# Layer 1's edges by pairs of groups, with PSUM banks given by hand and the last groups in conditional blocks

## The chip, the core and the metric

The program runs on one core of a Trainium2 chip. The core has a matmul engine (TensorE; PE in the profile, its weight loads PEld), a vector engine (VectorE, DVE), an activation engine (ScalarE, ACT), a general engine that also gathers (GpSimd, POOL), and a sync engine that issues transfers (SyncE, SP). They run side by side, each through its own instructions in order, and meet at semaphores. Matmul results land in PSUM, eight banks of 512 f32 columns on 128 partitions; everything else lives in SBUF.

The metric is the device time of one execution in microseconds. Three timed runs of the kernel before took 2873.72, 2878.11 and 2884.48 us; the median is 2878.11.

## The reference

Four layers, each a graph layer and a feed-forward layer, on 1250 nodes of 512 features, 20000 edges, f32. Only two parts bear on the change. Layer 0's graph layer is a convolution that here goes through the matrix of edge counts between nodes. Layer 1's is an attention over edges with four heads:

```python
h = (x @ W).reshape(n, H, C)
a_src = (h * att_src[None]).sum(-1)
a_dst = (h * att_dst[None]).sum(-1)
alpha = a_src[src] + a_dst[dst] + a_edge
alpha = jax.nn.leaky_relu(alpha, NEG_SLOPE)
amax = jax.lax.stop_gradient(jax.ops.segment_max(alpha, dst, num_segments=n))
ex = jnp.exp(alpha - amax[dst])
denom = jax.ops.segment_sum(ex, dst, num_segments=n)
att = ex / (denom[dst] + 1e-16)
msg = h[src] * att[:, :, None]
out = jax.ops.segment_sum(msg, dst, num_segments=n).reshape(n, H * C) + bias
```

The sources are drawn evenly. The destinations are drawn as `1250 * uniform ** 2` and sorted, so low-numbered nodes get most of the edges.

## The kernel before, in words

**Groups.** `grouped` sorts the edges into groups of `GS` = 512, none of which crosses the border between two blocks of `P` = 125 destination nodes. There are ten blocks (`NT`); the number of groups of each depends on the data, so the program has room for `NG` = 49 groups, and a block's last group is filled up with records that match no node. Groups past the last real one are all filler; they run like the others. For each group `bgrp` holds the number of its block, which engines read into a register. `ES` holds the records (source, destination, edge features), four to a partition and group; SyncE loads them group by group, with 49 transfers of 16 KB, and only then the big part of X.

`grouped` has a conditional block already (L1933 and L1934: a value is loaded into a register of GpSimd, VectorE and TensorE, and the block is skipped if it is zero). It is skipped when the destinations come sorted, as they do.

**Counts, in `l0_gnn`.** For each group VectorE compares destination and source with a row of node numbers (`onehots`, L202 and L205), and TensorE multiplies the two (`counted`, L211) into three PSUM banks that run on over all groups; ScalarE copies the running state (L216). Between the groups stand the statistics of the node features (`stats`, L219 and L220, VectorE, one of ten blocks at groups 8 to 17), `scales` at group 18, and the projection of a block (`projected`, L231 to L240) at every third group from 21 on. The order of this stage is not given by hand: a planner in the framework orders each engine's instructions by the program's order and by when it expects their inputs.

**Edges, in `l1_edges`.** For each group:

- `gathers` (L389 by a helper): GpSimd gathers 512 rows of the table `t1` (four times 128 rows) into `G`, one of six buffers.
- `onehot` (L1614), `pieces` (L1622 to L1628): VectorE makes the one-hots of the destinations and splits the source part of the score into three bf16 pieces, in `CD` beside the bits of the destination.
- `turned`: TensorE turns `CD` (L1635) and the one-hots (L1638); ScalarE copies both out (L1640, L1642).
- `spread` (L1650), `maxima` (L1657 to L1669): TensorE spreads the scores of a head over nodes and edges, VectorE takes the maximum over a group's edges per node and head, updates the running maximum `AM`, and makes `co`, the factor by which older sums shrink.
- `fetched` (L1677), `weights_of` (L1684 to L1688): TensorE brings the maximum back to the edges, VectorE and ScalarE form `ex`.
- `scaled` (L1694, L1697): a quarter of `G` is multiplied by `ex` on VectorE, three quarters on ScalarE.
- `summed` (L1704), `added` (L1713): TensorE sums per node into two banks, VectorE shrinks and adds into `ACC`.

The loop at the end of the function writes out the order in which VectorE, ScalarE and TensorE take these steps for groups at different stages (`manual_schedule`). Each step takes its PSUM banks from a rotation of eight, nine banks a group.

**Around it.** `wst`, a pool of four 8 KB buffers a partition, streams weights for all layers and stands open over the whole program. `l1_start` prepares the edges while layer 0's feed-forward part runs; `l1_gnn` runs the edges, then divides, normalises and routes on.

Of the kernel before, what the change touches and what calls it, by code (L numbers as in the profile page):

```python
# [27 lines left out]
NG = 49  # L28
# [7 lines left out]
class Net:  # L36
# [5 lines left out]
    def __init__(self, ctx, tc, a):  # L42
# [3 lines left out]
        self.wst = ctx.enter_context(tc.tile_pool(name="wst", bufs=4))  # L46
        c = self.consts = ctx.enter_context(tc.tile_pool(name="consts", bufs=1))
        self.flip = 0
# [20 lines left out]
    def pool(self, ctx, name, bufs=1, side=None):  # L69
        return ctx.enter_context(self.tc.tile_pool(name=name, bufs=bufs, side=side, reuse_waits="tile"))  # L70

# [81 lines left out]
    def l0_gnn(self, done):  # L153
# [6 lines left out]
        with ExitStack() as ctx:  # L160
# [6 lines left out]
            with ExitStack() as c2:  # L167
# [76 lines left out]
                for g in range(NG):  # L244
                    if g % 8 == 1:
                        local(g + 1, min(g + 9, NG))
                    if g + 1 < NG:
                        onehots(g + 1)
                    counted(g)
                    if g == 0:  # L250
                        arrived()
                    if 8 <= g < 8 + NT:
                        stats(g - 8)
                    if g == 8 + NT:
                        scales()
                    if g > 18 and g % 3 == 0 and g // 3 - 7 < NT:
                        projected(g // 3 - 7)
# [344 lines left out]
    def l1_start(self, ctx):  # L602
# [11 lines left out]
        f.norm = Norm(self, ctx, "g1n", side="right", bufs=2)  # L614
# [4 lines left out]
        nc.gpsimd.dma_start(wet, a["L1_gnn_W_edge"])  # L619
        wa = p.tile([128, 4, 2 * nh], F32, name="g1wa")  # L620
# [66 lines left out]
    def l1_gnn(self, nxt):  # L687
# [3 lines left out]
        ACC = self.g1.ACC  # L691
        with ExitStack() as c2:
            self.l1_edges(c2)
        done = self.l1_route(nxt)
# [845 lines left out]
    def edge_bits(self):  # L1540
# [9 lines left out]
        with ExitStack() as c3:  # L1550
# [15 lines left out]
            bt = r.tile([128, nb], F32, name="g1bt")  # L1566
            for b in range(nb):
                y = r.tile([128, ST], I32, name=f"g1y{b}")
# [17 lines left out]
    def l1_edges(self, ctx):  # L1586
# [8 lines left out]
        gq = self.pool(ctx, "g1g", bufs=6)  # L1595
        q4 = self.pool(ctx, "g1h", bufs=4)
        q = self.pool(ctx, "g1s", bufs=3)

        st = {}

        def gathers(g):
            G = gq.tile([128, 4, tw], F32, name="G")
            ix, o = SI, 4 * g
            if g in (2, 3):

                ix, o = q.tile([128, 4], I32, name="ix"), 0
# [5 lines left out]
        def onehot(g):  # L1612
            oh = q4.tile([128, 4, P], F32, name="oh")
            nc.vector.tensor_tensor(oh, self.iota[:, None, :P].to_broadcast([128, 4, P]),  # L1614
                                    ES[:, 4 * g:4 * g + 4, 1:2].to_broadcast([128, 4, P]), OP.is_equal)
            st[g]["oh"] = oh

        def pieces(g):

            t0, v = 4 * g, st[g]  # L1620
            s = q4.tile([128, 4, nh], F32, name="s")
            nc.vector.tensor_tensor(s, v["G"][:, :, nh * (ch + 1):], AE[:, t0:t0 + 4, :], OP.add)  # L1622
            c = [CD[:, t0:t0 + 4, nr + j * nh:nr + (j + 1) * nh] for j in range(3)]
            nc.vector.tensor_copy(c[0], s)
            rest = q.tile([128, 4, nh], F32, name="rest")
            nc.vector.tensor_tensor(rest, s, c[0], OP.subtract)
            nc.vector.tensor_copy(c[1], rest)
            nc.vector.tensor_tensor(c[2], rest, c[1], OP.subtract)  # L1628
            v["s"] = s

        def turned(g):
            t0, v = 4 * g, st[g]
            pc = self.psum.tile([128, 1024], BF16, name="cd_ps", tag="b")
            for k in range(4):
                nc.tensor.transpose(pc[:nr + 3 * nh, k * 128:(k + 1) * 128], CD[:, t0 + k, :], identb)  # L1635
            ps = self.bank("oht_ps")
            for k in range(4):
                nc.tensor.transpose(ps[:P, k * 128:(k + 1) * 128], v["oh"][:, k, :], self.ident)  # L1638
            R = q.tile([nr + 3 * nh, GS], BF16, name="R")
            nc.scalar.copy(R, pc[:nr + 3 * nh, :GS])  # L1640
            ohT = q.tile([P, GS], F32, name="ohT")
# [552 lines left out]
```

## Time and profile before

| | |
|---|---|
| median of three runs | 2878.11 us |
| lowest, highest | 2873.72, 2884.48 us |
| profiled execution, its own time | 2880.85 us |
| its span, first to last instruction | 2879.0 us |
| PE busy | 2526.9 us (88%) |
| DVE busy | 1501.2 us (52%) |
| ACT busy | 834.5 us (29%) |
| POOL busy | 495.3 us (17%) |
| mean granted clock of PE | 0.91 |
| ES loads, first to last issue | 20.65 to 75.4 us |
| counts, first to last matmul | 25.0 to 192.8 us |
| edges, first gather to the first instruction behind the loop | 850.4 to 1312.5 us |

Busy times are of the whole span and say little of a stage; the shares of a stage are read from the view of busy time by stretches, and the order of events in a round from the timeline. In the timeline a square bracket says how long the engine stood idle before the instruction, and what released it. The granted clock is the share of full speed at which the throttle lets TensorE run; a matmul at half clock takes about twice as long.

### The profile page before, as it was taken

What the parts mean: (1) busy time and instruction counts of PE and PEld (TensorE: products, weight loads), DVE (VectorE), ACT (ScalarE), POOL (GpSimd) and SP (SyncE); (2) the same over time, 40 slices, a digit from 0 to 9 for tenths busy, and PEclk for the clock granted to TensorE, in tenths of its full rate; (3) what the DMA queues carried; (4) which work ended last, traced back from release to release, by engine and by line L of the source; (5) the groups of instructions that cost most, each with busy time, mean ns of one, the idle gap of its engine ahead of it and who ended that gap; (6) DMA issues with size and microseconds to landing.
All of it is one profiled execution on the core that took longest, in us unless ns stands there. A gap on an engine that the chain in (4) does not pass through costs nothing. (4 is left out here: it accounts for less than half of the span.)

```text
span 2879.0 us, 30656 instructions
## 1 busy us (share of the span) xinstructions
PE 2526.9 (88%) x10610; PEld 1598.9 (56%) x10610; DVE 1501.2 (52%) x3571; ACT 834.5 (29%) x1855; POOL 495.3 (17%) x550
## 2 busy tenths in 40 slices
PE   6799879999787888887769899999999799859896
PEld 3455679999645666665544455445544334445442
DVE  8676632000146888886234998547963554631000
ACT  4451011121124555554122244013421221211110
POOL 0012111120014444430220000100000111122211
PEclk9999679999886888887789899999999899979998
DMA  1212336666424444440773210401122202259997
GB/s 35 92 36 77 88 125 200 207 211 200 115 67 130 119 119 120 119 90 26 259 253 122 71 36 24 141 32 37 64 65 88 81 0 64 83 196 357 361 372 250
DMA packets 109897, 369.50 MB, mean 128 GB/s; under 512 B 35040, under 2 KB 39925, under 8 KB 87467
## 3 DMA queue, kind: packets, MB, share of 16 engines
q1 hardware_dynamic: 60875, 257.91, 25.5%
q0 software_dynamic: 44848, 101.55, 13.8%
q10 hardware_dynamic: 4015, 8.06, 0.9%
q8 instruction: 84, 1.38, 0.2%
q14 instruction: 75, 0.61, 0.1%
HBM read 337.83 MB, written 29.53 MB: 128 GB/s over the span
## 5 line engine op out<-in xcount | busy, mean ns | idle before, releaser
L1076 PE MATMUL g_acc<-g_e,g2hh 125*128 125x417 f32 (+1 forms) x960 | 345.3, 520 | 7.5 <-DVE g_e L1066 7.5
L1076 PEld LDWEIGHTS g_acc<-g_e,g2hh 125*128 125x128 f32 x960 | 183.1, 192 | 167.3 <-issue 157.7
L389 POOL DMA_INDIRECT G<-t,SI x188 | 186.1, 990 | 345.0 <-issue 284.9
L1704 PE MATMUL ac_ps<-G,oh 128*125 128x258 f32 x784 | 230.2, 457 | 0.0
L1704 PEld LDWEIGHTS ac_ps<-G,oh 128*125 128x125 f32 x784 | 175.7, 230 | 58.7 <-PE mx_ps L1650 20.1
L1518 PE MATMUL f_ps<-f3wd,f3ht 128*39 128x512 f32 (+1 forms) x704 | 177.0, 619 | 26.2 <-DMA f3wd<-in_L_ffn_W_down_dram 26.0
L536 PE MATMUL f_acc<-f0ht,f0w 128*128 128x187 f32 x1024 | 169.1, 328 | 13.5 <-ACT f0ht L528 13.5
L1697 ACT ACTIVATE G<-G,ex 128x129 f32<-128x129 f32 x588 | 177.7, 389 | 1.7 <-ACT ex L1688 0.2
L536 PEld LDWEIGHTS f_acc<-f0ht,f0w 128*128 128x128 f32 x1024 | 167.0, 194 | 14.1 <-ACT f0ht L528 13.8
L525 PE MATMUL f_ps<-f0xgt,f0w 128*128 128x187 f32 x1024 | 168.6, 324 | 0.1
L525 PEld LDWEIGHTS f_ps<-f0xgt,f0w 128*128 128x128 f32 x1024 | 165.3, 191 | 0.4 <-DVE f0xgt L95 0.3
L1060 DVE SCALAR_TENSOR_TENSOR g_e<-g_qb,g_a 125x1250 f32<-125x1250 f32 x80 | 120.4, 1515 | 68.4 <-DMA g_qb<-g_qd 60.8
L1524 DVE TENSOR_SCALAR f3y<-f_ps,f3k_wsel 39x512 f32<-39x512 f32 x32 | 24.0, 749 | 247.1 <-PE f_ps L1518 246.6
L1061 ACT ACTIVATE g_e<-g_e,g_a 125x1250 f32<-125x1250 f32 x80 | 106.2, 1335 | 137.9 <-DVE g_e L1060 137.7
L211 PE MATMUL c_ps<-ohs,ohd 128*125 128x512 f16 (+1 forms) x588 | 115.4, 348 | 28.3 <-DVE ohs L205 14.1
L1032 PE MATMUL g_ps<-g22w,g2ht 128*125 128x512 f32 x320 | 137.8, 592 | 0.0
L1003 DVE CUSTOM_DVE_ANT_0 g_junk<-g_mb,g_asb 125x1250 f32<-125x1250 bf16 x80 | 116.6, 1457 | 20.1 <-DMA g_asb<-g_as 16.6
L1518 PEld LDWEIGHTS f_ps<-f3wd,f3ht 128*39 128x39 f32 (+1 forms) x704 | 44.7, 120 | 141.7 <-issue 97.7
L1657 DVE TENSOR_REDUCE gm<-mx_ps 125x1 f32<-125x512 f32 x196 | 121.3, 680 | 2.4 <-PE oht_ps L1638 2.4
L1066 DVE SCALAR_TENSOR_TENSOR g_e<-g_e,CT 125x1250 f32<-125x1250 f32 x80 | 115.8, 1450 | 7.3 <-ACT g_e L1061 7.1
L549 DVE TENSOR_SCALAR f0y<-f_ps,f0xg,f0r 128x512 f32<-128x512 f32 (+1 forms) x16 | 12.2, 802 | 203.6 <-PE f_ps L547 203.6
L211 PEld LDWEIGHTS <-ohd 128*125 128x125 f16 x588 | 74.8, 139 | 69.5 <-issue 29.1
(655 smaller groups left out, 4029.4 us busy)
## 6 DMA issues: line engine op xcount, KB each, us to landing
f3wd<-in_L_ffn_W_down_dram SPq DMA_DIRECT2D x64, 1280.0 KB
f0w<-in_L_ffn_w_dram SPq DMA_DIRECT2D x64, 1024.0 KB
f1w<-in_L_ffn_w_dram SPq DMA_DIRECT2D x17, 1024.0 KB
f3wu<-in_L_ffn_W_up_dram SPq DMA_DIRECT2D x16, 1024.0 KB
g_mb<-mbd POOLq DMA_DIRECT2D x40, 305.2 KB
g_qb<-g_qd SPq DMA_DIRECT2D x16, 625.0 KB
f2tv<-in_L_ffn_tv_W_dram SPq DMA_DIRECT2D x16, 512.0 KB
wa_w<-in_L_gnn_WT_dram SPq DMA_DIRECT2D x6, 1024.0 KB
```

Source lines behind the costliest of these rows:

```text
L211: nc.tensor.matmul(pss[i][:P, :cn], lhsT=ohd[g % 2][:, k, :], rhs=ohs[(4 * g + k) % R][:, c0:c0 + cn], start=g == 0 and k == 0, stop=k == ...
L389: self.nc.gpsimd.indirect_dma_start(out=out, out_offset=None, in_=table, in_offset=bass.IndirectOffsetOnAxis(ap=idx, axis=0))
L525: nc.tensor.matmul(ps[:, :cap], lhsT=w[:, k, f * 128:(f + 1) * 128], rhs=xgt[e][:, k, :], start=k == 0, stop=k == 3)
L536: nc.tensor.matmul(acc[e][d][:, :cap], lhsT=w[:, f, d * 128:(d + 1) * 128], rhs=ht[e][:, 4 * c + f, :], start=c == 0 and f == 0, stop=c == ...
L1003: nc.vector.tensor_tensor_reduce(junk, mb, asb[h], 1.0, -3e38, OP.add, OP.max, accum_out=mx[:, i, h:h + 1])
L1032: nc.tensor.matmul(ps[:P, :], lhsT=HT[:, k, i * P:(i + 1) * P], rhs=ws[hf][k // 4][:, k % 4, :], start=k == 0, stop=k == kt - 1)
L1060: nc.vector.scalar_tensor_tensor(e, qb[h][0], A8[:, s, h:h + 1], qb[h][1], OP.add, OP.max)
L1076: nc.tensor.matmul(accs[h][f][c][:, :cn], lhsT=H[:, s, h * 256 + f * 128:h * 256 + (f + 1) * 128], rhs=e[:, c0:c0 + cn], start=s == 0, sto ...
L1518: nc.tensor.matmul(ps[64 * h:64 * h + k, :], lhsT=ht[g][:n, f, j * k:(j + 1) * k], rhs=ws[h][:n, f - f0, :], start=f == 0, stop=f == nf - 1)
L1657: nc.vector.tensor_reduce(gm[:, h:h + 1], v["mx"][h][:P, :], AX.X, OP.max)
L1697: nc.scalar.activation(gv[:, k, h], gv[:, k, h], AF.Copy, scale=v["ex"][:, k, h:h + 1])
L1704: nc.tensor.matmul(v["ac"][j][:P, 0:2 * (ch + 1)], lhsT=v["oh"][:, k, :], rhs=v["G"][:, k, j * 2 * (ch + 1):(j + 1) * 2 * (ch + 1)], start ...
```

## The change

1. `NG` becomes 50 and a new `NM` is 46. The loop of the counts runs over 46 groups; groups 46 to 49 stand behind it in a conditional block (`rest`), which is entered only if there are more than 46 groups (`more`, two new VectorE instructions in `grouped`). The same for the edges.
2. In the counts the statistics stand at groups 14 to 23, `scales` at 24, the projections at every second group from 26 on.
3. In the edges the loop runs over 23 pairs of groups. Banks are given once: four for the maxima, two for the sums (`ac`), one for the codes of both groups (`pc`), one for the turned one-hots (`tr`); what `fetched` brings back (`mg`) lies in columns 320 to 383 of the first `ac` bank. `pieces`, `coded`, `lowered` and `weights_of` work on a pair at once; `maxima` has two VectorE instructions fewer, and `co` is made by Relu and Exp on ScalarE. Of a pair's eight quarters VectorE scales one and ScalarE seven. `G` has nine buffers.
4. `wst` closes before the edges and opens again behind them (`wst2`), and the norm of `l1_start` closes as well; `edge_bits` takes two buffers in turn.

```diff
-NG = 49
+NG = 50
+NM = 46
...
+    def stream(self, name):
+        self.wctx = ExitStack()
+        self.wst = self.pool(self.wctx, name, bufs=4)
...
-                for g in range(NG):
+                for g in range(NM):
...
-                    if g + 1 < NG:
+                    if g + 1 < NM:
                         onehots(g + 1)
                     counted(g)
                     if g == 0:
                         arrived()
-                    if 8 <= g < 8 + NT:
-                        stats(g - 8)
-                    if g == 8 + NT:
+                    if 14 <= g < 14 + NT:
+                        stats(g - 14)
+                    if g == 14 + NT:
                         scales()
-                    if g > 18 and g % 3 == 0 and g // 3 - 7 < NT:
-                        projected(g // 3 - 7)
+                    if g > 25 and g % 2 == 0 and g // 2 - 13 < NT:
+                        projected(g // 2 - 13)
+                ET = mybir.EngineType
+                with self.rest([ET.PE, ET.DVE, ET.Activation]):
+                    for g in range(NM, NG):
+                        onehots(g)
+                        counted(g)
...
+        self.g1.ctx.close()
+        self.wctx.close()
         with ExitStack() as c2:
             self.l1_edges(c2)
+        self.stream("wst2")
...
+        gq = self.pool(ctx, "g1g", bufs=9)
+        q8 = self.pool(ctx, "g1h", bufs=8)
+        q4 = self.pool(ctx, "g1p", bufs=4)
+        q = self.pool(ctx, "g1s", bufs=2)
+        mx = [self.bank(f"mx_ps{h}") for h in range(nh)]
+        ac = [self.bank(f"ac_ps{j}") for j in range(2)]
+        pc = self.psum.tile([128, 1024], BF16, name="cd_ps", tag="b")
+        tr = self.bank("oht_ps")
+        mg = ac[0][:, 320:320 + 16 * nh].rearrange("p (k h) -> p k h", k=8)
...
+        def maxima(g):
+            v, w = st[g], pr[g // 2]
+            if "co" not in w:
+                w["co"] = q4.tile([P, 2, nh], F32, name="co")
+            gm = q.tile([P, 1, nh], F32, name="gm")
+            for h in range(nh):
+                nc.vector.tensor_reduce(gm[:, 0, h:h + 1], mx[h][:P, :], AX.X, OP.max)
+            b = v["b"] = nc.vector.value_load(self.bgrp[0:1, g:g + 1], min_val=0, max_val=NT - 1)
+            M = AM[:, ds(b, 1), nh:]
+            nc.vector.tensor_tensor(gm, gm, AM[:, ds(b, 1), 0:nh], OP.add)
+            nc.vector.scalar_tensor_tensor(gm, gm, 0.2, gm, OP.mult, OP.max)
+            nc.vector.tensor_tensor(w["co"][:, g % 2:g % 2 + 1, :], gm, M, OP.subtract)
+            nc.vector.tensor_tensor(M, M, gm, OP.max)
+            mn = v["mn"] = q4.tile([P, 1, 2 * nh], F32, name="mn")
+            nc.vector.tensor_copy(mn, AM[:, ds(b, 1), :])
...
+            for i in range(-2, NP + 1):
+                if i >= 0:
+                    for j in range(2):
+                        one(gathers, i + 3, j)
+                one(spread, i + 1, 0)
+                at(weights_of, i)
+                one(scaled, i, 0, range(1, 4))
+                one(maxima, i + 1, 0)
+                one(scaled_v, i, 0, 0)
+                one(summed, i - 1, 0)
+                one(spread, i + 1, 1)
+                one(added, i - 1, 0)
+                one(scaled, i, 1, range(0, 2))
+                one(turned, i + 1, 0)
+                one(scaled, i, 1, range(2, 4))
+                one(summed, i - 1, 1)
+                one(maxima, i + 1, 1)
+                if i < 0:
+                    ...
+                else:
+                    at(pieces, i + 2, 0, 2)
+                    for j in range(2):
+                        one(onehot, i + 2, j)
+                one(turned, i + 1, 1)
+                at(coded, i + 2)
+                for j in range(2):
+                    one(fetched, i + 1, j)
+                at(lowered, i + 1)
+                one(added, i - 1, 1)
+        with self.rest([E.PE, E.DVE, E.Activation, E.Pool]):
+            for i in range(NP, NG // 2):
+                ...
+    def rest(self, engines):
+        E = mybir.EngineType
+        flag = self.nc.values_load(self.more[0:1, 0:1], engines=engines, min_val=0, max_val=NG - NM)
+        return self.tc.If(flag != 0)
...
+        nc.vector.tensor_tensor(self.more, start[0:1, NT - 1:], ng[0:1, NT - 1:], OP.add)
+        nc.vector.tensor_scalar(self.more, self.more, NM, -NM, OP.max, OP.add)
```

## The prediction

> **What bounds the kernel now.** Three stages of one core are touched: the counts of layer 0 (25 to 194 us of the span), layer 1's edges (850.4, the first gather, to 1312.5, the first instruction behind the loop: 462.1 us), and what little lies between them. I read the 40 slices first (edges at DVE 8 or 9 tenths, PE 8 or 9, clock 8 or 9), then the busy time by stretches. The columns are stretch, length, then busy us of PE, PEld, DVE, ACT, POOL with their counts, granted clock, DMA share, GB/s.
>
> ```profile
> 950.00:1000.00 50.00, 43.77 (x200) 32.48 (x200) 42.09 (x147) 30.08 (x94) 21.07 (x23) 0.86 0.45 120
> 1000.00:1050.00 50.00, 43.52 (x201) 32.57 (x202) 40.57 (x144) 27.35 (x83) 21.58 (x22) 0.83 0.42 112
> 1050.00:1100.00 50.00, 42.70 (x196) 32.26 (x196) 42.76 (x148) 29.95 (x94) 22.19 (x23) 0.86 0.46 127
> ```
>
> No engine is full; PE runs at a mean 0.86 of its clock. 890 to 1300 us hold 46 groups: 410/46 = 8.91 us a group. The chain of waits in those 410 us says who hands over to whom (total, times, longest):
>
> ```profile
> PEld L1635 <- DVE g1cd L1628: 73.4, 40, 4.0
> PE cd_ps L1635 <- DVE g1cd L1628: 57.4, 34, 3.6
> DVE ex L1684 <- PE mg_ps L1677: 23.7, 40, 1.6
> DVE g1acc L1713 <- PE ac_ps L1704: 5.1, 6, 1.2
> ```
>
> DVE makes a group's pieces, PE waits for them, turns them, fetches the maxima, DVE waits for those. A group's pieces in the timeline (start, length, engine, line, operation), one group at half clock and the next at full:
>
> ```profile
> 1005.86 5.28 PE L1704 MATMUL ac_ps<-G,oh 128*125 128x258 f32 x16
> ...
> 1010.74 1.57 DVE L1713 SCALAR_TENSOR_TENSOR g1acc<-g1acc,co,ac_ps 125x129 f32 x4
> 1011.06 0.40 PE L1635 MATMUL cd_ps<-g1id,g1cd 128*27 128x128 bf16 x4
> 1011.39 0.70 PE L1638 MATMUL oht_ps<-ident,oh 128*125 128x128 f32 x4
> 1011.93 0.96 PE L1677 MATMUL mg_ps<-mn,ohT 125*128 125x8 f32 x8
> 1012.82 1.07 PE L1650 MATMUL mx_ps<-R,g1sel 27*125 27x512 bf16 x4
> 1012.92 0.17 DVE L1684 TENSOR_TENSOR ex<-s,mg_ps 128x16 f32<-128x16 f32 x1 [0.62 <-PE mg_ps L1677]
> 1013.82 3.75 PE L1704 MATMUL ac_ps<-G,oh 128*125 128x258 f32 x16
> 1014.00 3.63 ACT L1697 ACTIVATE G<-G,ex 128x129 f32<-128x129 f32 x12
> 1014.61 2.48 DVE L1657 TENSOR_REDUCE gm<-mx_ps 125x1 f32<-125x512 f32 x4
> ```
>
> By starts (each to the next) a group at full clock costs PE 0.33 + 0.43 + 0.99 + 1.00 + 3.75 = 6.5 us and DVE 0.83 (weights) + 0.62 (scaling) + 2.40 (reductions) + 0.94 (small ones) + 0.60 (one-hots) + 1.04 (pieces) + 1.57 (adding) = 8.0.
>
> For the counts and for a conditional block, three lines:
>
> ```profile
> 18.27 0.18 DVE L1924 TENSOR_SCALAR bgrp<-gb 1x49 int32<-1x49 f32 x1 [0.71 <-DVEq L1934]
> ...
> 86.51 1.29 DVE L219 BATCH_NORM_STATS2 g_st<-X 125x6 f32<-125x512 f32 x2 [7.88 <-DMA X<-in_x_dram]
> ...
> 93.63 6.13 PE L211 MATMUL c_ps<-ohs,ohd 128*125 128x512 f16 x22 [13.63 <-DVE ohs L205]
> ```
>
> A skipped block cost DVE 0.71 us; the node statistics wait 7.88 us for X, and PE loses 13.63 behind them.
>
> **Part 1, groups 47 to 50 conditional.** The draw has expected edges per block of 125 nodes of 20000(sqrt((b+1)/10) - sqrt(b/10)); in groups of 512 that is 13+6+4+4+3+3+3+3+3 and 2 or 3, so 44 or 45, and the blocks are skipped. Edges lose three groups, 3 x 8.91 = 26.7 us (inside the sum of part 2). Counts lose three at 2.41 us (distance of L202's starts, 46.3, 48.8 ... 58.7): -7.2. Against it: the last projection, which now runs on PE while DVE builds the first count block, moves into the loop; three groups with one projection take 10.6 us (166.45 to 177.05), so it costs 10.6 - 7.2 = +3.4. One more load of ES on SP (35 in 39.14 us) puts X's load 1.1 us later: +1.1. The skip is bounded by 0 (an engine that waits anyway) and, as the new blocks hold several times the code of L1934's, by five times its row, 3.6; I take the row itself, +0.7 in each stage. Code behind a block can't be moved ahead of it: at 1311 to 1313 that is DVE's small f1nid and f1lt, under 1 us.
>
> **Part 2, pairs.** Per pair DVE drops four weight instructions (0.83, the other four are 32 wide: +0.04), one scaling (0.62), four pieces (0.8), and about 0.1 of the small ones: 16.0 - 2.3 = 13.7. PE's work stays 13.0 at full clock. ACT gets 28 scalings for 24 (3.63/12 each, 8.5) + copies 0.59 x 2 + 1.0 + exponentials and Relu 0.64 = 11.3. POOL's eight gathers are 8 x 1.26 = 10.1; nine buffers let the second group's start once the first sum of the round is through, a round ahead of need. So no engine fills 16 us; the order decides.
>
> The order by hand: `mg` lies in the bank of `ac[0]`. I take it that waits are set by bank and not by column (if by column: rival a). Then added(i-1,1), written behind fetched, waits for the fetch though it reads other columns; behind it on DVE stand the next weights and maxima, and the next sums on PE wait for both. One round, in line: weights 0.87, first sums 3.75, first adding 1.57, second sums 3.75 (they reuse the banks), turned 0.43, wait for the pieces 0.27, coded 0.66, two fetches 1.98, second adding 1.57, five handovers of 0.06: **15.1 us at full clock**, of which 10.57 are PE's path (3.75 x 2 + 0.43 + 0.66 + 1.98). ACT's copies (R at 14.2) and spread lie beside it.
>
> The clock: bounds are 1.0 (15.1 us a round) and 0.76, the lowest of a 200 us stretch with edges (1200:1400): 10.57/0.76 - 10.57 = +3.3, 18.4. I take the stage's own 0.86: +1.7, **16.8**. The nearest row speaks for it: PE is without sums for 4.9 us a group now (1017.57 to 1022.5) and would be for 5.9 a round. In one-microsecond stretches (columns as above) the clock reads 0.50 from 1003 to 1009, 1023 to 1026 and 1040 to 1046, after waits of PE of only 2.1 to 2.6 us and the light work behind them:
>
> ```profile
> 1003.00:1004.00 1.00, 1.00 (x6) 0.97 (x6) 0.00 (x0) 0.15 (x1) 0.70 (x2) 0.50 0.71 175
> 1009.00:1010.00 1.00, 1.00 (x6) 0.87 (x5) 0.97 (x5) 0.21 (x1) 0.00 (x0) 1.00 0.00 0
> 1023.00:1024.00 1.00, 1.00 (x4) 0.81 (x3) 1.00 (x2) 1.00 (x4) 0.22 (x1) 0.50 0.69 216
> ```
>
> The Trainium skill, "TensorE: Matmul & The Clock Gate", Part 1 (the HAM clock gate), says that the clock halves after an idle window of some 3.4 us; in the new round PE never idles over 1.6 us, so by the page the round would be 15.1 and the edges 394 us; the rows, where the clock fell after shorter waits, count for more.
>
> Filling: first pair's gathers and transfer, 15.5 (10.1 + 2.9 to land, pieces and turning 2.5); the first maxima and second pair's pieces on a cold PE, 20; a round without sums, 16.5: 52. Then 21 full rounds x 16.8 = 353, one without new maxima 14, the last sums and addings 11. 52 + 353 + 25 = 430, against 462.1: **-32**.
>
> **Part 3, statistics six groups later.** The text puts statistics 0 at group 8, the trace after 22 one-hots: the planner put them where it expects X. Group 14 is still ahead of that place, so I take 0 (ends: 0 and -7.9, the whole wait). The DVE time of the statistics (10 x 0.66 in a row) is paid in either place.
>
> **Part 4, memory and the rest.** wst closes over the edges: SP's next weight load is f1w at 1387.5, behind a wait for f1inc of 539.6 us, so nothing that loads early now is lost: 0 (end: +2). G may take g1w's place, last read at 846.0, before the first gather. Relu and Exp: L1119 and L1061 alternate with one table load, so none is added. Two DVE instructions for `more`: +0.4.
>
> Sum against the profiled execution (2880.85; span 2879.0): counts -7.2 + 3.4 + 1.1 + 0.7 = -2.0; edges -32 + 0.7; +0.4; together -33: 2848. That execution lies 2.7 over the median 2878.1, so 2845.
>
> **Rivals.** (a) The shared bank makes no wait, or the clock stays full. Without the bank wait the path is DVE's 13.7 a round: 52 + 288 + 25 = 365, -97, so 2780; with it but at full clock 394, -68, 2809. For it: PE's idle stretches get shorter. Against: fetched and added stand in that order in the code. (b) Slower, by the clock alone: from 0.76 down (break-even is (462 - 77)/21 = 18.3 us a round) pairs lose; at 0.70, 19.6 a round, 489 us, +27, so 2904. For it: one unbroken light stretch of 5.9 us a round instead of 4.9 a group. Against: 9.2 us of near-unbroken sums follow it, 4.8 now. (c) The statistics do move and X is there: -8 more, 2837, inside (main). (d) The blocks are entered: four groups unpipelined at 15 to 20 us, twice partly, +30 at least, 2880 or more; the draw speaks against it. (e) The pairs gain nothing over single groups: the round is 17.8, -12 with part 1 and its filling, 2866.
>
> **Numbers.** Main with (c) 0.53, alone 2820 to 2860; (a) 0.19; (e) 0.10, half of it within 0.5%; (b) 0.13, of it 0.02 within; (d) and the unforeseen 0.05, of it 0.02 within. Range 2785 to 2885: some 0.07 of (a) lies below, and 0.12 of (b) and (d) above. A measurement of this kernel tells 0.5% (14 us) from no change: faster 0.53 + 0.19 + 0.05 = 0.77, same 0.05 + 0.02 + 0.02 = 0.09, slower 0.14.
>
> **To look for afterwards.** First gather to the den instruction: 430 us. Spacing of the first sums of two pairs: 16.8, and just before adding a wait for mg's matmuls; without it (a). Clock in the loop: 0.86, under 0.76 is (b). Statistics: 7.9 us of DVE waiting for X again. No instruction with 47th-group data; DVE idle at the skips under 2 us. The prediction is wrong if the round is limited by something not in the line above, as a queue of POOL or ACT.

## The result and the profile after

The change made the kernel slower: 2917.85 us (2915.91 to 2920.28, four runs) against 2880.25 (2873.72 to 2884.48, four runs), a ratio of 1.0133 with a 95% interval of 1.0111 to 1.0155. The prediction was 2845, with 2785 to 2885 as its range.

The two profiled executions differ by 39.5 us (spans 2879.0 and 2918.5). Three marks in the timelines divide that:

| stretch | before | after | difference |
|---|---|---|---|
| start to the first gather | 850.38 | 858.55 | +8.2 |
| first gather to `g1den` behind the loop | 462.1 | 495.7 | +33.6 |
| from there to the end | 1566.5 | 1564.2 | -2.3 |

So the loop that was to be 32 us shorter is 33.6 longer. Busy time by stretches of after, columns as in the prediction:

```profile
950.00:1000.00 50.00, 37.49 (x159) 27.70 (x159) 31.19 (x95) 26.66 (x83) 17.32 (x18) 0.71 0.38 104
1000.00:1050.00 50.00, 40.63 (x186) 30.48 (x186) 32.48 (x100) 28.54 (x89) 20.59 (x21) 0.78 0.38 102
1050.00:1100.00 50.00, 37.29 (x174) 27.73 (x171) 29.54 (x90) 24.19 (x74) 19.12 (x20) 0.73 0.40 113
```

DVE fell from 42 of 50 us to 31. With 17.8 us for two groups before and 20.5 for a pair now, that is 14.9 us of work a pair before and 12.7 after: the work that the change removes did go. But PE fell as well, from 43 to 38 of 50 us, and its clock from 0.85 to some 0.74 (means of these three stretches). Nobody is busier, so a new wait must have come. The chain of waits from 920 to 1300 us (total, times, longest) names it:

```profile
POOL G L401 <- ACT G L1718: 186.4, 18, 10.6
DVE g1acc L1737 <- PE mx_ps L1670: 55.5, 11, 5.2
DVE g1acc L1737 <- remote: 34.1, 7, 5.0
PE mx_ps L1670 <- issue: 34.1, 16, 3.1
ACT R L1660 <- remote: 33.8, 8, 4.5
```

"remote" is a releaser that the view could not name. L1737 is `added`, L1660 the copy of the turned codes to `R`. Both wait for TensorE, for longer than TensorE works. One round's end in the timeline:

```profile
1105.83 0.95 POOL L401 DMA_INDIRECT G<-t,SI  x1 [10.17 <-ACT G L1718]
...
1111.30 0.62 PE L1658 MATMUL cd_ps<-g1id,g1cd 128*27 128x128 bf16 x8 [0.66 <-DVE rest L1652]
1111.85 1.95 PE L1698 MATMUL ac_ps<-mn,ohT 125*128 125x8 f32 x16
1114.79 0.95 POOL L401 DMA_INDIRECT G<-t,SI  x1 [0.30 <-issue]
1115.79 1.00 ACT L1660 COPY R<-cd_ps 27x1024 bf16<-27x1024 bf16 x1 [4.53 <-remote]
1116.84 1.86 PE L1670 MATMUL mx_ps<-R,g1sel 27*125 27x512 bf16 x4 [3.04 <-issue]
1117.33 1.50 DVE L1737 SCALAR_TENSOR_TENSOR g1acc<-g1acc,co,ac_ps 125x129 f32 x4 [4.92 <-remote]
```

The reader is to see four things. The eight transposes into `cd_ps` end at 1111.92, and ScalarE's copy of them, which needs nothing else and stands idle, starts at 1115.79: 3.87 us later. The fetch ends at 1113.80, and the second adding starts at 1117.33: 3.53 later. PE then stands idle for 3.04, since its next work needs `R`. And POOL issues its eight gathers in one unbroken row, from 1105.83 to 1115.74, across all of it. In the last three rounds, with four gathers and then none, the same adding starts 0.04 us behind the fetch, and the rounds last 17.10, 16.70 and 15.72.

Are the matmuls themselves late, with their records wrong? In eleven of the rounds five signals of PE come within 0.14 us of one another, 34 ns apart (from 1137.70, for instance), while the records spread the work behind them over some 3 us (1134.3 to 1137.0). The four matmuls into `mx_ps` alone take 1.86 us, so they can't have ended within 0.14: in these rounds the work was done and its signals came late. In the others, the round shown among them, the traces leave both open. "Late signals" below means the distance from a recorded end to the start of the waiting instruction.

### The profile page after: what moved, and what is told of

Read it like the earlier page. It is cut to its first block, busy times and chain, and to the rows that moved or that the text cites. A ratio compares the mean times of both kernels' runs of the same rounds, so it can differ in the third digit from the quotient of the medians.

```text
span 2918.5 us, 30026 instructions
## 1 busy us (share of the span) xinstructions
PE 2516.5 (86%) x10466; PEld 1590.5 (54%) x10466; DVE 1427.9 (49%) x3191; ACT 828.0 (28%) x1844; POOL 476.4 (16%) x538
## 5 line engine op out<-in xcount | busy, mean ns | idle before, releaser
L1728 PE MATMUL ac_ps<-G,oh 128*125 128x258 f32 x736 | 221.9, 466 | 39.0 <-DVE ex L1706 37.3
L401 POOL DMA_INDIRECT G<-t,SI x168 | 164.4, 979 | 371.6 <-ACT G L1718 186.4
L1728 PEld LDWEIGHTS ac_ps<-G,oh 128*125 128x125 f32 x736 | 169.5, 237 | 93.6 <-DVE ex L1706 54.0
L1718 ACT ACTIVATE G<-G,ex 128x129 f32<-128x129 f32 x644 | 193.9, 390 | 2.1 <-issue 1.3
L1737 DVE SCALAR_TENSOR_TENSOR g1acc<-g1acc,co,ac_ps 125x129 f32 x184 | 64.2, 349 | 147.4 <-PE mx_ps L1670 55.8
L1679 DVE TENSOR_REDUCE gm<-mx_ps 125x1 f32<-125x512 f32 x184 | 113.9, 680 | 2.9 <-issue 2.3
```

The source lines that it names most:

```text
L401: self.nc.gpsimd.indirect_dma_start(out=out, out_offset=None, in_=table, in_offset=bass.IndirectOffsetOnAxis(ap=idx, axis=0))
L1679: nc.vector.tensor_reduce(gm[:, 0, h:h + 1], mx[h][:P, :], AX.X, OP.max)
L1718: nc.scalar.activation(gv[:, k, h], gv[:, k, h], AF.Copy, scale=ex[:, k, h:h + 1])
L1728: nc.tensor.matmul(ac[j][:P, 0:2 * (ch + 1)], lhsT=v["oh"][:, k, :], rhs=v["G"][:, k, j * 2 * (ch + 1):(j + 1) * 2 * (ch + 1)], start=k == ...
```

## The experiments

**Single groups, or pairs?** The loop over pairs is put back to the one over single groups, everything else of the change stays.

```diff
-            for i in range(-2, NP + 1):
+            for g in range(-2, NM + 1):
 ...                                      # the steps of the kernel before
+        with self.rest([E.PE, E.DVE, E.Activation, E.Pool]):
+            for g in range(NM, NG):
+                ...
```

> Layer 1's loop as it was before, group by group, but with 46 groups and the rest in a conditional block; counts, statistics and memory as in the change. It prices the pairs alone against the change, and the rest of the change alone against the kernel before. If the pairs are what loses, the edges are 462.1 - 3 x 8.91 + 1 = 436 us, the start of the edges 4 to 8 us later than before, and the whole 2855 to 2865, faster than both. If the conditional block itself is what loses, it stays at 2890 or more.

Measured: 2854.74 us (2852.38 to 2856.63), ratio to before 0.9902 (0.9883 to 0.9921); edges 440.0. Dropping three groups is worth 22 us in the edges. The change takes 63 us longer than this kernel, 55.7 of them in the edges, which is more than its whole loss: the loss sits in the pairs.

**The row of gathers moved.** In the change a pair's two times four gathers stand at the round's top; their waits are for buffers: the second group's for this round's first sums, the next pair's first group's for its second sums, so they join to eight in a row. Here they are tied to two small DVE copies of their indices.

```diff
-                if i >= 0:
-                    for j in range(2):
-                        one(gathers, i + 3, j)
...
                 one(scaled_v, i, 0, 0)
+                if i >= 0:
+                    one(gathers, i + 3, 0, True)
...
                 one(added, i - 1, 1)
+                if i >= 0:
+                    one(gathers, i + 3, 1, True)
```

> The eight gathers of a pair no longer run in one row: four are tied to an index copy of DVE behind the first scaling of the round, four to one behind the round's last adding, so that POOL pauses between them. Theory 1 (the row of eight holds up the round): in the trace of the change ACT's copy of the codes starts 1.7 to 4.5 us after the last transpose and DVE's second adding some 3.5 us after the fetch's modelled end, in every round but the last two, which have four gathers and none and take 16.7 us. Then those two waits go, the round is 16 to 17.5 us instead of 20.4, the edges are 20 x 3.4 = 68 us shorter, the whole about 2850. Theory 2 (the light part of the round lowers the clock, and the clock alone makes the 20.4): the round stays at 20, the clock at 0.75, the whole within 10 us of 2918.

Measured: 2860.76 (2860.64 to 2861.29), ratio 0.9923 (0.9905 to 0.9941); edges 441.3, a round 17.68. The gathers did not split as meant: they are still eight in a row (1099.10 to 1109.18), but some 7 us earlier in the round. There the late signal meets another waiter:

```profile
1105.86 0.70 PE L1664 MATMUL oht_ps<-ident,oh 128*125 128x128 f32 x4
1106.97 0.95 POOL L401 DMA_INDIRECT G<-t,ix  x1 [0.30 <-issue]
1108.99 0.58 ACT L1666 COPY ohT<-oht_ps 125x512 f32<-125x512 f32 x1 [3.71 <-remote]
...
1113.64 1.50 DVE L1737 SCALAR_TENSOR_TENSOR g1acc<-g1acc,co,ac_ps 125x129 f32 x4 [1.42 <-PE ac_ps L1698]
```

Transposes recorded up to 1106.56, their copy at 1108.99. The second adding is on time (0.04 us behind the fetch in every round); in all eighteen rounds with eight in a row it is this copy that is late, by 0.6 us or more. The lateness followed the row, and it costs less there, as the copy has slack.

**Two rows of four.** As above, with the first four tied behind `added(i - 1, 0)` instead.

> The first four gathers of a pair are tied to an index copy of DVE behind the first adding of the round, the other four to one behind the second, so that they come as two rows of four with a pause of some 3 us, as before the change. In the run with eight still in one row but seven us earlier the late completions of TensorE were still there, only on a copy of ACT that has slack. Theory 1a (the length of the row): four in a row hold nothing up, as in the loop before; no copy waits over 1 us for TensorE longer than its work, the round is 15.1 to 16.5 us, the whole 2835 to 2858. Theory 1b (any gather whose bytes come in under the turning and the fetch holds them up): the four now lie under just these, the two waits come back, the round is 18 to 20 us, the whole 2880 to 2915.

Measured: 2850.57 (2842.41 to 2855.22), ratio 0.9885 (0.9864 to 0.9906); edges 429.0, a round 17.10. The same end of a round as above:

```profile
1103.77 0.96 POOL L401 DMA_INDIRECT G<-t,ix  x1 [3.62 <-ACT ohT L1666]
1107.73 0.62 PE L1658 MATMUL cd_ps<-g1id,g1cd 128*27 128x128 bf16 x8 [0.85 <-DVE g1cd L1654]
1108.28 1.95 PE L1698 MATMUL ac_ps<-mn,ohT 125*128 125x8 f32 x16
1108.38 1.00 ACT L1660 COPY R<-cd_ps 27x1024 bf16<-27x1024 bf16 x1 [0.88 <-PE cd_ps L1658]
1110.27 1.50 DVE L1737 SCALAR_TENSOR_TENSOR g1acc<-g1acc,co,ac_ps 125x129 f32 x4 [1.42 <-PE ac_ps L1698]
...
1112.69 0.95 POOL L401 DMA_INDIRECT G<-t,ix  x1 [3.60 <-DVE ex L1707]
```

The adding starts 0.04 us behind the recorded end of the fetch, in place of 3.53. That holds for the adding in every round. `R` is on time in the round shown, but in most rounds it still starts 0.7 to 1.3 us behind its transposes, which costs PE 0.4. Same bytes, same eight gathers a round, a pause of some 3.6 us between them: 66.7 us of the edges gone. The pause also moved the rows: here the first ends at 1109.09, ahead of the fetch's end at 1110.23, so this run alone doesn't tell the length of a row from its place. The kernel before helps: from 915 us on 40 of its fetches end under a row of four, 0.7 to 4.2 us into it, and DVE starts at most 0.31 us behind them.

**The shared bank.** `mg` moves from the first `ac` bank to the second, so that the adding of the first two heads need not wait for the fetch.

```diff
-        mg = ac[0][:, 320:320 + 16 * nh].rearrange(...)
+        mg = ac[1][:, 320:320 + 16 * nh].rearrange(...)
```

> The fetched maxima lie in the second bank of the sums and not in the first. By my forecast the adding waits for the fetch because of the shared bank: then the adding of the first two heads runs beside the fetch, 0.8 us a round are saved, 18 us in all, about 2900. By theory 1 the fetch itself is late, the weights wait for it in either case, and the round stays at 20.4 (2905 to 2925). By theory 2 no change.

Measured: 2903.34 (2894.51 to 2910.46), ratio 1.0068 (1.0047 to 1.009); edges 483.7, 12.0 less than the change's, a round about 19.95. The late signals stay.

> The same with the fetched maxima in the second bank of the sums, which took 15 us off the change in its own order (two heads are added beside the fetch). Theory 1a: another 0.7 us a round, 12 to 18 us under the run with the pause alone, 2820 to 2845. Theory 1b: 2865 to 2900. If TensorE is what sets the round once nothing is held up, the gain is under 5 us.

Measured, both edits together: 2824.62 (2809.56 to 2830.69), ratio 0.9796 (0.9777 to 0.9816); edges 400.8, 28.2 less than with the pause alone, a round 15.87. The first two heads' adding now runs beside the fetch:

```profile
1100.13 1.95 PE L1698 MATMUL ac_ps<-mn,ohT 125*128 125x8 f32 x16
1100.63 0.72 DVE L1737 SCALAR_TENSOR_TENSOR g1acc<-g1acc,co,ac_ps 125x129 f32 x2
1102.12 0.73 DVE L1737 SCALAR_TENSOR_TENSOR g1acc<-g1acc,co,ac_ps 125x129 f32 x2 [0.77 <-PE ac_ps L1698]
```

A wait by bank is there, as predicted; over 22 rounds it is worth 0.55 us a round while signals are late, 1.28 when they are not.

**Bytes, or the row?** Several runs took bytes away from the gathers, and the first two are easily misread. All runs of this part but e13 are single executions.

```diff
-            G = gq.tile([128, 4, tw], F32, name="G")
+            G = Gs[g % 9]                     # nine fixed buffers
...
+                if g < 9 or g >= NM:
                     self.gather(G[:, k, :], t1, ...)
+                else:                         # rows of 4, later of 260 numbers
+                    self.gather(G[:, k, 0:nh], t1.rearrange("n (a b) -> (n a) b", b=nh)[0:N], ...)
```

> From the tenth group on a gather fetches four numbers of a row instead of 520: as many gathers at the same places, hardly any bytes, so the sums are not the reference's. If the bytes on the way into memory hold up the round, it falls to 16 to 17.5 us and the whole to about 2850. If POOL's issuing of eight in a row does it, the round stays at 20.4 and the whole at 2918. If the clock does it, the same, with the clock at 0.75.

Measured: 2859.24, edges 444.8, a round 17.09. The second adding is on time in every round; `R` is 1.5 to 1.6 us late in five of them, although a gather now brings 2 KB. In the filling, ahead of the first thin gather, the late signals are worse than in the change: `R` starts at 905.09, 14.08 us behind its transposes.

> From the 10th group on a gather fetches 260 of the 520 numbers of a row of the table, as rows of their own (other rows, so the sums are not the reference's); eight gathers a round in one row at the change's places, half the bytes (some 133 KB a gather). If it is the rate of bytes that holds TensorE's finish signals back, no late signals: a round of about 17 us, edges about 430 to 445, about 2860 us. If any row of eight gathers with bytes that a wait of TensorE's followers shares does it, a round of about 20.4 and about 2918. In between (a round of 18 to 19.5) it is in proportion to bytes.

Measured: 2848.87, a round 17.0, no late signals, in the filling neither. That reads like "bytes do it, with a threshold above half". The list of POOL's issues says otherwise: in both kernels they come as four and four, with POOL idle for 2.4 to 3.2 us between the rows and then for 4.4 to 4.5. The fixed buffers made the two rows, not the bytes. With them a gather is issued ahead of the sums that read its buffer's old rows and no longer waits for them, so that these kernels sum wrong rows for one group of each pair, whatever they fetch (this holds for the next four too). So the cross was run: all bytes with fixed buffers, and the quarters in reverse order, which was to make the row whole again.

> The change with nine fixed buffers in place of nine that rotate, and nothing else: a gather then waits only for the sums that read its own quarter of the buffer, so that the two groups of a round come as four and four with a pause of some 2 us, as they did in the runs with fewer bytes, but with all their bytes. If the unbroken eight are what holds TensorE's signals back: no late signals, a round of 17.1, edges about 430 to 445, 2845 to 2865. If the bytes are, whatever the places: a round of about 20.5 and 2905 to 2920.

> The same fixed buffers, but a group's four gathers issued from the last quarter to the first: the first of them waits for the last of the sums, as with rotating buffers, and eight come in one row again, with all their bytes. If the row is the cause: late signals again, a round of about 20.5, 2905 to 2925. If the rotating buffers did something else: about 17 and 2850 to 2865.

> Half the bytes a gather from the 10th group on (other rows, so the sums are not the reference's), fixed buffers, the quarters from the last to the first: eight in a row at the change's places with half the bytes. If bytes hold the signals back: late ones go or shrink, a round of 17 to 19. If the row of eight alone does: about 20.5 and 2905 to 2920.

> The same with four numbers a row from the 10th group on (the sums are not the reference's): eight in a row with next to no bytes. If the issuing by POOL alone holds the signals back: a round of about 20.5 and 2905 to 2920. If bytes are needed: no late signals, about 17.1 and 2850 to 2865.

Measured: 2850.32 (2843.31 to 2850.96; before on the same chip 2868.99, ratio 0.9933, 0.9906 to 0.9959), 2850.92, 2847.17, 2850.8; rounds 17.0 in all four, edges 430.5 to 431.1. Reversing did not join the rows: all four have four and four, so e14 to e16 did not make the test they were built for. What they do show is that with four and four, on one chip, the time does not depend on the bytes at all: e13, with every byte,

```profile
1106.98 0.95 POOL L401 DMA_INDIRECT G<-t,SI  x1 [2.04 <-PE ac_ps L1729]
...
1110.23 0.62 PE L1659 MATMUL cd_ps<-g1id,g1cd 128*27 128x128 bf16 x8 [0.47 <-DVE g1cd L1655]
...
1110.78 1.95 PE L1699 MATMUL ac_ps<-mn,ohT 125*128 125x8 f32 x16
1110.89 1.00 ACT L1661 COPY R<-cd_ps 27x1024 bf16<-27x1024 bf16 x1 [0.50 <-PE cd_ps L1659]
1112.77 1.50 DVE L1738 SCALAR_TENSOR_TENSOR g1acc<-g1acc,co,ac_ps 125x129 f32 x4 [1.42 <-PE ac_ps L1699]
```

has `R` 0.04 and the adding 0.04 us behind the recorded ends. That these five runs (e12 to e16) are on time can't be put down to four and four alone. They ran on two chips on which the kernel before takes 2870.40 and 2868.99, against 2879.40 to 2885.03 on the others, and the change itself was not run there. Up to the 37th gather e4 and e12 are the same program: e4 has `R` 14.08 us late under its row of 36 (855.78 to 901.14), e12 has it 0.04 behind the transposes under its row of forty (855.40 to 906.22). Here is e4, then e12:

```profile
890.41 0.60 PE L1662 MATMUL cd_ps<-g1id,g1cd 128*27 128x128 bf16 x4 [7.09 <-DVE ix L1631]
905.09 1.00 ACT L1664 COPY R<-cd_ps 27x1024 bf16<-27x1024 bf16 x1 [19.71 <-remote]
```

```profile
881.88 0.60 PE L1662 MATMUL cd_ps<-g1id,g1cd 128*27 128x128 bf16 x4 [0.65 <-DVE g1cd L1658]
882.53 1.00 ACT L1664 COPY R<-cd_ps 27x1024 bf16<-27x1024 bf16 x1 [4.55 <-PE cd_ps L1662]
```

So something besides the kernel, the chip perhaps, has a part in it. On the chips where late signals occur, four and four stand in e4, e5, e6 and e9, where the second adding doesn't wait for a late fetch and `R` is up to 1.6 us late outside the filling; the change (run again below) and e3, on the same chips as e9 and e4, have `R` 2 to 5.5 us late.

The missing corner, a row of eight with fewer bytes, needs the change's rotating buffers with their waits:

```diff
-            G = gq.tile([128, 4, tw], F32, name="G")
+            G = gq.tile([128, 4, 260], F32, name="G")      # heads 0 and 1
+        Gf = gf.tile([128, 9, 4, 2 * (ch + 1)], F32, name="Gf")   # heads 2 and 3: constants
...
-                self.gather(G[:, k, :], t1, ...)
+                self.gather(G[:, k, :], t1.rearrange("n (a b) -> (n a) b", b=260)[0:N], ...)
```

> Rotating buffers and their waits as in the change, eight gathers in one row at the change's places; but a gather fetches 260 of a row's 520 numbers, the first two heads', from other rows, and the other two heads are scaled and summed from nine fixed blocks of constants (so the sums are not the reference's; DVE's scaling becomes two instructions, +0.1). If the bytes hold TensorE's signals back: late signals gone or about halved, a round of 17 to 19, 2850 to 2890. If the unbroken row of eight does it whatever it carries: R's copy some 1.5 to 4 us behind the transposes again, a round of about 20.5, 2905 to 2925.

Measured: 2922.7, a round 20.4, edges 495.3. Eight in a row (1089.66 to 1099.77), and the late signals are back with half the bytes:

```profile
1095.30 0.62 PE L1661 MATMUL cd_ps<-g1id,g1cd 128*27 128x128 bf16 x8 [0.40 <-issue]
...
1095.85 1.95 PE L1701 MATMUL ac_ps<-mn,ohT 125*128 125x8 f32 x16
...
1098.81 0.96 POOL L401 DMA_INDIRECT G<-t,SI  x1 [0.30 <-issue]
1100.30 1.00 ACT L1663 COPY R<-cd_ps 27x1024 bf16<-27x1024 bf16 x1 [4.40 <-remote]
1101.13 1.50 DVE L1744 SCALAR_TENSOR_TENSOR g1acc<-g1acc,co,ac_ps 125x129 f32 x4 [4.71 <-remote]
```

In e17 the second adding starts 2.75 to 3.42 us behind the fetch in all eighteen rounds with eight in a row. So neither the bytes nor the number of gathers a round decides, but how they lie: eight in a row across the handovers make the second adding late, four and four do not. Whether the rotating buffers' waits have a part in it no run shows, since no row of eight was had with fixed buffers.

**The counts.** First the edges of e2 with before's counts (49 groups, statistics at 8, projections at every third group, no conditional block there); then e2 with the tenth projection behind the block.

> Layer 1's loop group by group with 46 groups (2854.7 us with the counts of the change), and counts, statistics and projections as before the change: 49 groups, no conditional block there. In the change TensorE is idle for 3.7 us at the end of the counts, where before it had the last projection, and then turns and multiplies 40 matmuls at half clock. If that is what the counts part costs, the first gather comes at 850 to 852 us again instead of 853.9 to 858.6, the first sum over neighbours starts at 199.8 and not at 202, and the whole is 2849 to 2852. If the later start of the edges comes from elsewhere (memory, norm tiles), the first gather stays at 854 to 858.

Measured: 2856.21 (2851.78 to 2861.24), ratio 0.9903 (0.9881 to 0.9924), first gather at 853.36, against 2854.74 and 853.90 in e2: no difference that can be told. The three groups that the counts save bring nothing that shows.

```diff
-                    if g > 25 and g % 2 == 0 and g // 2 - 13 < NT:
+                    if g > 25 and g % 2 == 0 and g // 2 - 13 < NT - 1:
                         projected(g // 2 - 13)
                 with self.rest([ET.PE, ET.DVE, ET.Activation]):
                     ...
+                projected(NT - 1)
```

> As the loop of single groups with 46 groups and conditional blocks, but the tenth projection stands behind the conditional block of the counts and not in their loop, so that TensorE works while DVE builds the first count block. If the idle TensorE and its clock cost the 4 us, the counts keep their three groups' gain: first gather at 846 to 850, the whole 2845 to 2850. If the block is in the way (TensorE waits at its branch for the others), nothing changes: 2852 to 2857.

Measured: 2849.5 (2844.53 to 2855.55), ratio 0.9877 (0.9854 to 0.99), first gather at 848.51. The interval overlaps those of e2 and e7, so the time alone does not show a gain. What changed stands in PE's timeline of the change and then of this kernel (C is the count matrix that DVE builds behind the counts):

```profile
196.68 4.56 PE L302 MATMUL ct_ps<-ident,C 125*125 125x125 f32 x20 [3.70 <-DVE C L294]
...
202.24 10.72 PE L310 MATMUL g_ps<-g0h,g0ct 125*125 125x512 f32 x20 [1.00 <-DVE g0h L284]
```

```profile
188.67 3.70 PE L246 MATMUL g_ps<-g0w,g0xt 128*125 128x512 f32 x8 [0.77 <-ACTq L266]
192.21 2.35 PE L303 MATMUL ct_ps<-ident,C 125*125 125x125 f32 x20
```

Before had the projection in front of the same transposes as well (2.35 us, multiplications from 199.76). Moved into the loop, it leaves PE 3.70 us idle there, and the 20 transposes and the first of the 20 matmuls behind run at half clock (granted 0.50 from 196 to 202 us, 0.66 from 202 to 208, then 1.00): 4.56 and 10.72 us for 2.35 and 8.75. With the projection behind the block the clock is 1.00 from 192 to 203.

**The best version, and how well times repeat.** The pause, `mg` in the other bank and the last projection behind the block:

> The pairs with the pause between the two rows of gathers, the fetched maxima in the second bank of the sums, and the tenth projection behind the conditional block of the counts. Theory 1a: the edges 400 us as without the last step (2824.6 us), the first sum over neighbours at 194.5 instead of 199.5 to 202; of these 5 to 7 us up to 5 reach the end: 2817 to 2824. If what is won in the counts is lost again to the clock behind them, it stays at 2822 to 2828.

Measured: 2813.99 (2812.29 to 2821.81, five runs), ratio 0.9764 (0.9743 to 0.9784). Its first gather comes at 846.63. Its edges take 409.7, 8.9 more than e6's and not the 400 expected; why is open.

> The change once more, unaltered. Up to the first gather the runs with the counts of the change are the same program, and that gather came at 848.6, 853.9, 854.9, 855.8, 857.2, 858.3 and 858.6 us. If the 8.2 us by which the change starts the edges later than before come from its counts, it is at 857 to 859 again; if they come from how the clock falls between 200 and 850, it is anywhere from 849 to 859. The edges take 495 us (490 to 500) either way.

Measured: 2914.91 (2912.02 to 2917.81), ratio 1.01 (1.0073 to 1.0127), edges 495.7 again, first gather at 856.33.

> The kernel before once more, unaltered, for the same question: first gather at 850.4 in its one profile so far. If that is a property of its counts, 849.5 to 851.5 again; if the clock decides, 845 to 857.

Measured: 2884.1 (2877.66 to 2888.35), ratio 0.9996 (0.9982 to 1.001), first gather at 852.94.

## Why the prediction was wrong, by its steps

**What bounds the loop: right for the rows read, and one row overlooked.** The profile of before already had a late signal, in the filling of the loop, under twelve gathers in a row (867.44 to 882.24):

```profile
878.40 1.71 PE L1677 MATMUL mg_ps<-mn,ohT 125*128 125x8 f32 x8
...
881.29 0.95 POOL L389 DMA_INDIRECT G<-t,SI  x1 [0.30 <-issue]
...
884.37 0.17 DVE L1684 TENSOR_TENSOR ex<-s,mg_ps 128x16 f32<-128x16 f32 x1 [7.57 <-remote]
```

The fetch ends at 880.11, its reader starts at 884.37, 4.26 later; the kernel before has it again in e11, with 4.20. I read only the steady rounds, where gathers come four at a time and signals are on time.

**Part 2, the round: this is the step that failed**, in two phrases: "five handovers of 0.06", and POOL's gathers at 10.1 us, "so no engine fills 16 us". I asked of POOL whether it has time for eight gathers, and it has. I did not ask where the row of eight falls and what it does to others. The handover from the fetch to the second adding measured 3.4 to 3.9 in the eighteen rounds with eight gathers, in place of 0.06. The prediction's own sign of being wrong, a limit "not in the line above, as a queue of POOL or ACT", came near it. The rest of the round's model held: with the adding on time edges were predicted at 430 and measured 429.0 (e5) and 430.5 (e13), a round at 16.8 and measured 17.0 to 17.1.

By terms, from the first gather:

| term | predicted | measured in after |
|---|---|---|
| filling, to the first weights of round 1 | 52 | 54.5 (858.55 to 913.01) |
| 21 rounds | 353 | 419.1 (18 x 20.53 + 17.10 + 16.70 + 15.72) |
| the rest | 25 | 22.2 |
| edges | 430 | 495.7 |

The 66 us are all in the second row: 3.15 us a round.

**The clock** was taken at 0.86. It is 0.76 in after (920 to 1240 us) and 0.80 in e5; the rows in which it reads 0.50 after short waits were the right ones to weigh. The page of the Trainium skill that I set against it, "TensorE: Matmul & The Clock Gate", Part 1, asks for an idle window of some 3.4 us; in e5 the clock falls in each light part of a round, though PE never idles there for over about 0.9 us:

```profile
1050.00:1100.00 50.00, 46.80 (x213) 35.26 (x213) 38.56 (x123) 31.89 (x99) 22.96 (x24) 0.80 0.45 124
```

Here the measurement decides against that row of the page. (The prediction also had PE idle for at most 1.6 us in the new round; in after it is idle for up to 3.5.) But the clock's loss against 0.86 would be 0.9 us a round by the prediction's own formula (10.57/0.80 less 10.57/0.86), and the round was only 0.2 to 0.3 longer; some other term was taken too high.

**The bank wait** was right in kind: e3 and e6 show it.

**Part 1** was predicted at -2.0 for the counts. The first gather of the profiled execution is 8.2 later. Over the profiled executions whose program is the same up to there, its place scatters from 848.6 to 858.6 with the change's counts (thirteen, mean 855.7) and from 850.4 to 853.4 with before's (three, mean 852.2): about +3.5, and e7 against e2 sees nothing. e8 and e9, with the last projection behind the block, lie at 848.51 and 846.63, below all thirteen. So -2.0 was wrong in sign or by a few us, and most of the 8.2 is scatter between programs that do the same. Its parts: three groups saved, but X lands 2.2 later (DVE's wait for it is 9.14 us against 7.88; 1.1 was predicted), and the moved projection costs PE 4.3 (its two rows, 0.59 + 3.70) and a slower clock behind it, where I had 3.4 and no clock. The blocks were skipped, as predicted; the one behind the edges costs 1.36 (last adding to 1352.91, `g1den` at 1354.27) for 0.7.

**Part 3**, the statistics: right. They still wait for X:

```profile
88.67 1.28 DVE L226 BATCH_NORM_STATS2 g_st<-X 125x6 f32<-125x512 f32 x2 [9.14 <-DMA X<-in_x_dram]
```

**Part 4**: right, as far as the noise lets one see. The stretch behind the edges is 2.3 us shorter, not longer; the kernel before alone scatters by more there (1566.5 us, and 1558.3 in e11).

**The rivals.** (a), no bank wait or a full clock: the wait is there; with it taken away (e6) the kernel comes to 2824.62, and to 2814 with e8's edit, well above the rival's 2780. (b), the clock alone makes it slower: its number is near (2904) and its sign right, but its mechanism is not the cause: at the 0.76 measured the prediction's formula gives 18.4 us a round, not 20.5, and the difference stands in the timeline as waits behind work that is recorded as ended. (c), statistics moved: no. (d), blocks entered: no. (e), pairs gain nothing: e5 with 2850.57 against e2 with 2854.74 says that pairs as written, with the adding on time, gain some 4 us, which their spread doesn't tell from nothing, and far less than their DVE work suggests, since the bank wait holds them back; with that gone too (e6) it is 30. The rival that was missing: a row of one engine's work that delays the signals of another.

**What stays open** is how the row does it. Bytes do not decide (e17, and e4's late `R` with 2 KB a gather). The row's length alone does not either: e4 and e12, the same program in the filling, are late and on time under rows of 36 and forty. Nor is it the loading of code, in the round shown: the DMA view of after from 1110 to 1118 has one queue only, the gathers' (packets, MB, share of 16 engines):

```profile
q0 software_dynamic: 492, 1.62, 71.7%
```

Two regularities stand in the timelines of the loop. The first is how far into a row a signal falls. In after the one-hots turned 0.9 and 4.8 us into a row are copied on time (0.15 us behind at most); `R`'s transposes and the fetches, which end 5.8 us into it or later, are late in every round. In e5 `R` is 1.2 us late when its transposes end 4.5 to 4.6 us into a row of four, while the one-hots, up to 4.0 us into it, are on time. In before and e11, filling aside, the fetches and turnings that end under a row, up to 4.5 us into it, are followed within 0.33. The second is when the wait ends. In all eighteen rounds of after with eight gathers the second adding starts 1.08 to 1.62 us behind the end of the eighth gather's issue; in e17 it is 1.17 to 1.64; in e5 a late `R` starts 1.00 to 1.08 behind the end of its row of four. So a row of four would be short enough and one of eight too long. That is read off, not tested, and it isn't the whole: `R` in after starts up to 3.2 us ahead of the row's end, and under the first sixteen gathers of after's filling it is on time (873.11) at the twelfth.

## What to carry to other kernels

When a change joins bursts of another engine's work, ask not only whether that engine has time for the burst but which handovers of others fall into it; a "remote" wait of several us in the filling of the old kernel, under just such a burst, is the price to take for them. Test a suspect by moving it before making it smaller: the runs that took bytes away also moved the gathers, and for a while told the wrong story. Watch on which chips the runs of a comparison were made: five runs here were on time on chips where no late signal was seen at all. And an instruction that lies between two stages may be worth more as cover for the clock than it costs.

## What was not expected of the hardware

- Signals of TensorE that reach other engines 1 to 5 us after the recorded end while GpSimd issues eight indirect gathers in a row of 10 us (after, e3, e10, e17). With the same eight as four and four (e5) the adding follows the fetch by 0.04 us, and `R` its transposes by 0.04 to 1.3. In the filling of e4 VectorE's own signals are late as well: four instructions of it (884.79 to 888.99), each of which reads what the one before wrote, wait 1.15 to 3.14 us each.
- The granted clock changes in the records only at multiples of 3.41 us, and some rounds settle on it: the change alternates 10.24 us at full and 10.24 at half clock (20.48 together; its round is 20.5), e5 10.24 and 6.83 (17.07; its round is 17.10). Those of e3 do not (17.96 to 21.07). A cut of less than a step may then bring nothing; that last sentence is an inference that no run here tests.
- Programs with the same first 850 us reach the first gather up to 10 us apart.
